# Graph attention by neighbour lists: a two-column copy ordered behind the norm factors' operation, and the first sort's triangle matmuls in the attention's PSUM tiles

## The chip, the cores and the metric

The kernel runs on one core of one Trainium2 chip. The metric is the device time of one execution in microseconds (us); smaller is better. Before the change three runs gave a median of 1821.51 us (1818.98 to 1823.71).

## What is computed

One layer of graph attention over 4096 nodes with 512 features, 8 heads of 64, and a dense 4096 x 4096 adjacency matrix of int32 in which a row holds some 9 ones on average. Cut to what matters:

```python
hs, ht = layer_norm(x), layer_norm(h_target)          # both [4096, 512]
q, k, v = ht @ Wq + bq, hs @ Wk + bk, hs @ Wv + bv    # 8 heads of 64
logits = where(adj != 0, q . k / 8, -1e30)            # per head
attn = softmax(logits) . v @ Wo + bo
ht = layer_norm(ht + attn)
ht = ht + gelu(ht @ W1) @ W2                          # 512 -> 2048 -> 512
out = layernorm(x + ht)
```

## The kernel before

The kernel does not form 4096 x 4096 logits. It turns each adjacency row into a short list of neighbours, sorts the rows by their number of neighbours, and for each tile of 128 rows gathers the keys and values of neighbour 0, 1, 2, ... from DRAM. A dense fallback (`general_path`) stands behind a flag at the end.

**The first stage** runs to about 300 us of the profile. Two kinds of work are interleaved in it.

- *Projections* (`project`, lines 864 to 960). For 16 groups of 256 rows of `x`: normalise (ScalarE, line 890), transpose on TensorE (line 904), scale into `hT` (ScalarE, line 914), multiply by Wk and Wv (TensorE, line 929), copy out of PSUM (ScalarE, line 931) and write 128 rows of keys and values to the DRAM table `kvd` (line 935, issued by ScalarE). An fp32 matmul appears in the profile as two passes.
- *Lists* (`edges`, lines 716 to 761). A row tile's adjacency comes in four quarters of 512 KB (line 713, issued by SyncE). ScalarE takes the sign of each entry (line 728), VectorE multiplies by an index and picks the largest by MAX8 (lines 733 and 735), then merges the candidates (lines 742 to 759) and SyncE writes the rest of them to DRAM (line 766). Each row tile has a record row with the degree, the row number, two norm factors and up to 24 neighbours (columns `DEG, TGT, ROW, RST, RST+1, E0...`).

After the first 16 row tiles (half "A") have lists, `prepare` calls `sort(0)` (lines 807 to 861): a counting sort by degree. A one-hot matrix `oh` of 48 bins is multiplied by a matrix of ones (line 838) for the running sums, which VectorE scans out of PSUM (line 839), and by a triangle `lower` (line 846) for the position inside a bin, which VectorE adds (line 847). The ranks come out of line 850, and GpSimd scatters the 16 record tiles by rank to DRAM (line 853). The second half of the rows, "B", is sorted during the attention by `sort(1)`, through the same lines.

**The attention stage** goes over 32 tiles of sorted rows. `prefetch` (line 979, on GpSimd) loads the sorted records of a tile into one of six `rec` buffers. `front` (lines 982 to 1016) gathers the target rows (line 966, GpSimd), copies degree and target row from the record to `tags` (line 993, VectorE, 128 x 2), applies a MAX with bypass to the two norm factors in the record (line 995, VectorE, in place), normalises with them (line 996, ScalarE), transposes (line 1000, TensorE), scales (line 1003, ScalarE), multiplies by Wq (line 1009, TensorE) and adds the bias (line 1014, VectorE). The operand `latest[-1]` on line 995 is not used in the value: it is there so that the operation comes after the tile it names, which is a `kvr` of the last two projection groups for the first two fronts and the logits `lg` of an attention step for the others. The attention itself gathers keys and values (line 966, 512 KB each), and multiplies by the query, reduces, exponentiates, weights and sums by TensorE transposes into the PSUM tile `cps` (lines 1218, 1223, 1227, 1182, 1190). `finish` divides and applies Wo (line 1113); `feed` is the feed-forward (lines 1323 and 1332); `end` normalises and scatters the output rows. `tags` is read by the gathers of `x` for the residual, by the output scatters (line 1300) and by `verdict` at the end of the attention.

**What sets the order.** `_weave` merges generators by the costs that they yield; that gives the order in which the program is written down. The build's scheduler then orders each engine's queue by its own model of times, moving instructions ahead where it takes their inputs to be there, unless an order is demanded. So a queue can hold an instruction long before its place in the text: the six copies of line 993 between 267 and 278 us belong to tiles 0 to 5, the operations of line 995 for tiles 2 to 5 come from 345 us on. An engine takes its queue in order.

**PSUM.** The pool `ps` has two tiles named `t` and two named `cps`[...]. In the first stage `t` is shared by the projections' transposes (line 899, every other pair of chunks) and the sort's matmuls; `cps` is used by the attention only.

Of the kernel before, what the change touches and what calls it, by code (L numbers as in the profile page):

```python
# [8 lines left out]
F32 = mybir.dt.float32  # L9
# [3 lines left out]
ALU = mybir.AluOpType  # L13
# [4 lines left out]
P = 128  # L18
# [359 lines left out]
DEG, TGT, ROW, RST, E0 = 0, 1, 2, 3, 5  # L378
# [65 lines left out]
def adj_resnorm_kernel(  # L444
# [33 lines left out]
    nc = tc.nc  # L478
# [54 lines left out]
    with tc.tile_pool(name="keep", bufs=1) as keep:  # L533
# [13 lines left out]
        tags = keep.tile([P, NT, 2], I32, name="tags")  # L547
# [3 lines left out]
        with ExitStack() as late:  # L551
# [3 lines left out]
            ps = late.enter_context(tc.tile_pool(name="ps", bufs=1, space=PSUM))  # L555
# [18 lines left out]
            def turn_of(name, places):  # L574
                turns[name] += 1
                return places[turns[name] % len(places)]
# [230 lines left out]
            def sort(part):  # L807

                i0, n = PARTS[part]
                me = slice(i0, i0 + n)  # L810
                pool, R = lp, Rs[part]
                nc.vector.tensor_reduce(deg[:, me], dpart[:, me, :], AX.X, ALU.add)
                nc.vector.tensor_copy(R[:, :, DEG], deg[:, me])
                dif, rank = tools[:, 928:928 + n], tools[:, 944:944 + n]
                ranki, b16 = tools[:, 960:960 + n].bitcast(I32), tools[:, 976:984].bitcast(BF16)
                nc.vector.scalar_tensor_tensor(dif, deg[:, me], float(RE), cnt[:, me], op0=ALU.min,
                                               op1=ALU.not_equal)
                nc.vector.tensor_reduce(bad[:, 1 + part:2 + part], dif, AX.X, ALU.max)
                nc.vector.tensor_scalar(dif, deg[:, me], 0.0, float(NB - 1), op0=ALU.max,
                                        op1=ALU.min)  # L820
                nc.vector.tensor_scalar(b16, dif, -1.0, float(NB - 1), op0=ALU.mult, op1=ALU.add)
                if part:
                    oh = turn_of("wide", wide).bitcast(BF16)
                else:
                    oh = wp.tile([P, NB * n], BF16, name="oh")
                oh = oh[:, :NB * n].rearrange("p (b i) -> p b i", b=NB)
                nc.vector.tensor_tensor(oh, b16.unsqueeze(1).to_broadcast([P, NB, n]),
                                        bins.unsqueeze(2).to_broadcast([P, NB, n]), ALU.is_equal)
                ohf = oh.rearrange("p b i -> p (b i)")
                pos = turn_of("wide", wide).bitcast(F32)  # L830
                pos = pos[:, :NB * n].rearrange("p (b i) -> p b i", b=NB)
                posf = pos.rearrange("p b i -> p (b i)")
                w = NB * n // 2
                yield 6.0
                for c in range(2):
                    sl = slice(c * w, (c + 1) * w)
                    pt = ps.tile([P, w], F32, name="t", bufs=2)
                    nc.tensor.matmul(pt, ones_bf, ohf[:, sl], start=True, stop=True)
                    nc.vector.tensor_tensor_scan(posf[:, sl], one_c.to_broadcast([P, w]), pt,
                                                 0.0 if c == 0 else posf[:, c * w - 1:c * w],  # L840
                                                 op0=ALU.mult, op1=ALU.add)
                yield 4.0
                for c in range(2):
                    sl = slice(c * w, (c + 1) * w)
                    pa = ps.tile([P, w], F32, name="t", bufs=2)
                    nc.tensor.matmul(pa, lower, ohf[:, sl], start=True, stop=True)
                    nc.vector.tensor_add(posf[:, sl], pa, posf[:, sl])
                nc.vector.tensor_mul(pos, pos, oh)
                nc.vector.tensor_reduce(rank, pos.rearrange("p b i -> p i b"), AX.X, ALU.add)
                nc.vector.tensor_copy(ranki, rank)  # L850
                yield 10.0
                for i in range(n):
                    ins = nc.gpsimd.indirect_dma_start(
                        out=recs_d[part][:, :],
                        out_offset=bass.IndirectOffsetOnAxis(ap=ranki[:, i:i + 1], axis=0),
                        in_=R[:, i, :], in_offset=None)

                    tc.declare_no_dep(ins.ins, group=f"scatter{part}", reason="other rows")
                    tc.add_to_no_dep_group(f"scatter{part}", ins.ins)
                    yield 3.0 if part else 1.3  # L860
                done.add(part)
# [101 lines left out]
            recs, tqs, h2Ts, done, ready, latest, newest = {}, {}, {}, set(), [], [], []  # L963

            def gather(dst, table, idx):
                nc.gpsimd.indirect_dma_start(  # L966
                    out=dst, out_offset=None, in_=table[:, :],
                    in_offset=bass.IndirectOffsetOnAxis(ap=idx, axis=0))
# [13 lines left out]
            def front(i, idle=0):  # L982


                rec = recs[i]
                tq = sp.tile([P, 2 * D], F32, name="tq", bufs=3)
                t = tq[:, :D]
                gather(t, h_target, rec[:, TGT:TGT + 1])
                for _ in range(1 + idle):
                    yield  # L990


                nc.vector.tensor_copy(tags[:, i, :], rec[:, DEG:TGT + 1])
                m = rec[:, RST:RST + 2].bitcast(F32)
                nc.vector.scalar_tensor_tensor(m, m, latest[-1], m, op0=ALU.bypass, op1=ALU.max)
                nc.scalar.activation(t, t, AF.Identity, bias=m[:, 1:2], scale=m[:, 0:1])
                yield
                pt = ps.tile([P, KC, P], F32, name="t", bufs=2)
                for kc in range(KC):
                    nc.tensor.transpose(pt[:, kc, :], t[:, kc * P:(kc + 1) * P], ident)  # L1000
                hT = tq[:, D:].rearrange("p (c t) -> p c t", c=KC)
                for kc in range(KC):
                    nc.scalar.activation(hT[:, kc, :], pt[:, kc, :], AF.Identity,  # L1003
                                         bias=b1r[:, kc:kc + 1], scale=s1c[:, kc:kc + 1])
                yield
                yield
                pq = ps.tile([P, D], F32, name="t", bufs=2)
                for kc in range(KC):
                    nc.tensor.matmul(pq, hT[:, kc, :], wq[:, kc, :], start=kc == 0,  # L1009
                                     stop=kc == KC - 1)  # L1010
                yield
                yield
                yield
                nc.vector.scalar_tensor_tensor(tq[:, :D], pq, HD ** -0.5, bqr,
                                               op0=ALU.mult, op1=ALU.add)
                tqs[i] = tq
# [32 lines left out]
            def begin(i, lead):  # L1049

                if i not in begun_fronts:
                    begun_fronts.add(i)
                    fronts[i] = front(i, 2 * lead + (2 if i > NA else 0))
                    step(fronts, i)
# [97 lines left out]
            def first_fronts():  # L1152

                for i in range(EARLY):
                    prefetch(i)
                for i in range(EARLY):
                    fronts[i] = front(i)
                    step(fronts, i)
                while not latest:
                    yield None  # L1160
                while fronts:
                    go_on()
                    yield 4.0
# [278 lines left out]
            def other_lists():  # L1442
                for cost in ed:
                    yield 1.5 * cost
                keep_rest()
                yield from sort(1)
# [38 lines left out]
```

## Time and profile before

| | |
|---|---|
| median of three runs | 1821.51 us (1818.98 to 1823.71) |
| the profiled execution's own time | 1820.38 us |
| its span, first to last instruction | 1818.6 us |
| TensorE (PE) busy | 1686.6 us, 93% of the span |
| VectorE (DVE) busy | 1435.0 us, 79% |
| ScalarE (ACT) busy | 1221.5 us, 67% |
| GpSimd (POOL) busy | 976.5 us, 54% |
| DMA | 463.26 MB, mean 255 GB/s |
| copy of line 993 | 32 times, median 168 ns |
| operation of line 995 | 32 times, median 212 to 218 ns |
| triangle matmul, line 846, first sort | 2 passes, 477 and 524 ns, at 235.8 and 237.8 us |

How to read it: "busy" adds up the instructions of an engine. In the lists of waits, "A <- B" means that engine A sat idle until B was done, and the number is that idle time. In the timeline a row has its start, its length, the engine, the line, the operation, tile written <- tiles read, a count, and in brackets the idle time just before it with what ended it. POOLq, SPq and ACTq are instructions that issue transfers, PEld is the loading of weights. In a table of stretches there are the busy time of each engine with its number of instructions, the clock that TensorE was granted (1.00 is full), the share of time in which the DMA engines were busy, and what they moved in GB/s.

### The profile page before, as it was taken

The page shows a single profiled execution, that of the slowest core. Times are in us where ns is not written, and L with a number is a line of the kernel's source. Part 1 is how long each engine was busy: PE and PEld are TensorE (multiplying, and loading weights), DVE is VectorE, ACT ScalarE, POOL GpSimd, SP SyncE. Part 2 cuts the span into 40 slices and gives each one's busy share as a digit, 9 for nine tenths or more (in the row PEclk, how much of TensorE's full clock was granted, in tenths as well). Part 3 has the DMA queues.
Part 4 walks back from the last instruction along what each step waited for, and adds up shares of the span by engine and source line. Part 5 has one row for each costly group of instructions (what it writes and reads, how often), then busy time and mean ns, then how long its engine had stood idle before and what let it go on. Part 6 is the DMA issues. An engine that isn't in the chain of part 4 may idle for free. (4 is left out here: it accounts for less than half of the span.)

```text
span 1818.6 us, 22965 instructions
## 1 busy us (share of the span) xinstructions
PE 1686.6 (93%) x7030; PEld 1100.9 (61%) x7030; DVE 1435.0 (79%) x2660; ACT 1221.5 (67%) x3119; POOL 976.5 (54%) x834
## 2 busy tenths in 40 slices
PE   7999975588999999999999989999999999999997
PEld 3444432466766666676776657666666666666664
DVE  6989866899999837787978989979879697988200
ACT  5867644486998645767878878877877576787311
POOL 1000143666465576676668788877575655764101
PEclk9999987598999999999999999999999999999999
DMA  9999958989887747677879878887786767774000
GB/s 345 366 389 370 346 171 304 405 284 324 292 303 234 238 141 269 227 267 263 289 259 316 296 258 277 261 291 266 241 268 206 262 222 242 247 248 152 18 6 26
DMA packets 140268, 463.26 MB, mean 255 GB/s; under 512 B 16500, under 2 KB 21672, under 8 KB 140136
## 3 DMA queue, kind: packets, MB, share of 16 engines
q0 software_dynamic: 96656, 342.64, 55.7%
q1 hardware_dynamic: 35664, 95.98, 15.0%
q10 hardware_dynamic: 7816, 23.08, 3.3%
q8 instruction: 58, 0.95, 0.2%
q14 instruction: 74, 0.61, 0.1%
HBM read 430.75 MB, written 30.89 MB: 254 GB/s over the span
## 5 line engine op out<-in xcount | busy, mean ns | idle before, releaser
L966 POOL DMA_INDIRECT kv<-kvd,rec x603 | 757.4, 1256 | 370.7 <-PE cps L1190 134.1
L1332 PE MATMUL po<-w,gt 128*128 128x512 f32 x1024 | 466.3, 598 | 6.6 <-ACT gt L1326 6.3
L1323 PE MATMUL pf<-h2T,w 128*128 128x256 f32 (+1 forms) x2176 | 466.5, 368 | 2.0 <-issue 1.7
L1323 PEld LDWEIGHTS pf<-h2T,w 128*128 128x128 f32 x2176 | 389.5, 191 | 66.9 <-issue 22.1
L1202 ACT ACTIVATE kv<-kv,pa 128x64 f32<-128x64 f32 x1520 | 391.0, 336 | 4.4
L1218 DVE TENSOR_TENSOR kv<-kv,tq 128x1536 f32<-128x1536 f32 (+2 forms) x211 | 352.0, 1678 | 51.0 <-DMA kv<-kvd,rec 48.4
L1223 DVE TENSOR_REDUCE lg<-kv 128x24 f32<-128x1536 f32 (+2 forms) x211 | 350.6, 1669 | 1.0
L1332 PEld LDWEIGHTS po<-w,gt 128*128 128x128 f32 x1024 | 188.9, 192 | 203.2 <-issue 195.2
L1190 PE MATMUL cps<-ident,kv 128*128 128x128 f32 x2008 | 267.5, 281 | 45.3 <-issue 22.7
L1190 PEld LDWEIGHTS cps<-ident,kv 128*128 128x128 f32 x2008 | 240.9, 146 | 112.7 <-issue 69.8
L1182 DVE TENSOR_TENSOR kv<-kv,p 128x1024 f32<-128x1024 f32 (+1 forms) x211 | 251.4, 1196 | 26.3 <-ACT p L1227 21.1
L687 POOL TENSOR_TENSOR n_rs<-n_ve,mhalf 128x2 f32<-128x2 f32 (+2 forms) x51 | 50.1, 983 | 329.8 <-DVE n_ve L680 154.5
L728 ACT ACTIVATE kv<-kv 128x1024 uint8<-128x1024 int32 x128 | 134.9, 1055 | 97.4 <-DMA kv<-in_adj_dram 49.3
L1326 ACT ACTIVATE gt<-pf 128x512 f32<-128x512 f32 x128 | 76.4, 597 | 97.1 <-PE pf L1323 74.9
L929 PE MATMUL pq<-wk,h2T 128*128 128x512 f32 x256 | 125.3, 634 | 12.3 <-ACT h2T L914 5.5
L735 DVE MAX8 cand<-kv 128x8 uint16<-128x103 uint16 (+1 forms) x640 | 133.6, 259 | 0.5
L1326 ACT ACT_TABLE_LOAD x103 | 132.1, 1283 | 1.7
L1009 PE MATMUL t<-wq,tq 128*128 128x512 f32 x256 | 117.4, 602 | 5.0 <-ACT tq L1003 4.3
L929 PE MATMUL pq<-wv,h2T 128*128 128x512 f32 x256 | 115.3, 593 | 0.6 <-ACT tq L931 0.6
L1113 PE MATMUL t<-wo,rb 128*128 128x512 f32 x256 | 115.2, 592 | 0.0
L1227 ACT ACTIVATE p<-lg 128x24 f32<-128x24 f32 (+2 forms) x179 | 39.1, 219 | 105.7 <-DVE lg L1223 83.3
L929 PEld LDWEIGHTS pq<-wk,h2T 128*128 128x128 f32 x256 | 50.4, 204 | 78.1 <-issue 59.0
(159 smaller groups left out, 1582.2 us busy)
## 6 DMA issues: line engine op xcount, KB each, us to landing
kv<-in_adj_dram SPq DMA_DIRECT2D x128, 512.0 KB
kvd<-tq ACTq DMA_DIRECT2D x24, 512.0 KB
kv<-kvd,rec POOLq DMA_INDIRECT x603
kv<-in_L_gnn_h_target_dram SPq DMA_DIRECT2D x32, 256.0 KB
kv<-in_x_dram SPq DMA_DIRECT2D x15, 512.0 KB
rest_d<-gid SPq DMA_DIRECT2D x32, 160.0 KB
w<-in_L_gnn_W_dram SPq DMA_DIRECT2D x4, 1024.0 KB
kvd<-kv ACTq DMA_DIRECT2D x8, 512.0 KB
```

What stands on the lines that cost most here:

```text
L728: nc.scalar.activation(sg, a, AF.Sign, accum_out=dpart[:, i, h:h + 1])
L735: nc.vector.max(cand[:, h * SQ + s, :], wd[:, w0:w1])
L929: nc.tensor.matmul(pkv, hT[:, kc, j * P:(j + 1) * P], w[:, kc, :], start=kc == 0, stop=kc == KC - 1)
L966: nc.gpsimd.indirect_dma_start(out=dst, out_offset=None, in_=table[:, :], in_offset=bass.IndirectOffsetOnAxis(ap=idx, axis=0))
L1182: nc.vector.tensor_tensor(v4, v4, p[:, j0:j0 + m, :].unsqueeze(3) .to_broadcast([P, m, H, HD]), ALU.mult)
L1190: nc.tensor.matmul(cps[:, c, :], kv[:, j, D + c * P:D + (c + 1) * P], ident, is_transpose=True, start=j0 + j == 0 and c == 0, stop=j0 + n ...
L1202: newest[:] = [nc.scalar.mul(v, v, pa[:, hd:hd + 1]).ins]
L1218: nc.vector.tensor_tensor(kv[:, :n, :D], kv[:, :n, :D], tq[:, :D].unsqueeze(1).to_broadcast([P, n, D]), ALU.mult)
L1223: nc.vector.tensor_reduce(lg[:, :n, :], kv[:, :n, :D].rearrange("p j (h d) -> p j h d", h=H), AX.X, ALU.add)
L1323: nc.tensor.matmul(pf[:, k, :], w1[(f0 + k) // KC][:, kc, (f0 + k) % KC * P:((f0 + k) % KC + 1) * P], h2T[:, kc, :w], start=kc == 0, stop= ...
L1326: nc.scalar.activation(gt, pf, AF.Gelu_apprx_tanh)
L1332: nc.tensor.matmul(po[j], gt[:, k, j * P:(j + 1) * P], w2[(f0 + k) // KC][:, (f0 + k) % KC, :], start=False, stop=f0 + k == FC - 1, skip_g ...
```

## The change

Two edits. In `front`, the copy of degree and target row (before: line 993, ahead of the operation on the norm factors) is written behind that operation and tied to it: `issue_after` adds an edge of order, on VectorE alone, from the operation to the copy. In `sort`, the PSUM tile of the triangle matmul takes the name `cps` in the first sort and keeps `t` in the second.

```diff
@@ sort
                     sl = slice(c * w, (c + 1) * w)
-                    pa = ps.tile([P, w], F32, name="t", bufs=2)
+                    pa = ps.tile([P, w], F32, name="t" if part else "cps", bufs=2)
                     nc.tensor.matmul(pa, lower, ohf[:, sl], start=True, stop=True)
                     nc.vector.tensor_add(posf[:, sl], pa, posf[:, sl])
@@ front
-                nc.vector.tensor_copy(tags[:, i, :], rec[:, DEG:TGT + 1])
                 m = rec[:, RST:RST + 2].bitcast(F32)
-                nc.vector.scalar_tensor_tensor(m, m, latest[-1], m, op0=ALU.bypass, op1=ALU.max)
+                tie = nc.vector.scalar_tensor_tensor(m, m, latest[-1], m, op0=ALU.bypass,
+                                                     op1=ALU.max)
+                with tc.issue_after(tie.ins):
+                    nc.vector.tensor_copy(tags[:, i, :], rec[:, DEG:TGT + 1])
                 nc.scalar.activation(t, t, AF.Identity, bias=m[:, 1:2], scale=m[:, 0:1])
```

## The prediction, written before the result

> **What bounds the kernel now.** I read the busy time by stretches first, because the shares of the whole span mix stages.
>
> ```profile
> 240.00:255.00 15.00, 15.00 (x42) 7.10 (x41) 12.66 (x55) 9.51 (x19) 9.49 (x10) 1.00 0.42 141
> 255.00:270.00 15.00, 10.72 (x31) 4.82 (x30) 3.05 (x18) 2.78 (x6) 10.80 (x14) 1.00 0.24 52
> 270.00:300.00 30.00, 25.68 (x56) 10.91 (x56) 22.40 (x99) 18.26 (x37) 3.73 (x5) 0.89 0.80 262
> 300.00:370.00 70.00, 28.42 (x124) 21.21 (x124) 55.70 (x84) 29.80 (x102) 48.44 (x39) 0.61 1.01 389
> 360.00:1740.00 1380.00, 1333.20 (x5970) 917.82 (x5969) 1139.65 (x1509) 992.42 (x2655) 886.03 (x734) 0.98 0.74 247
> 1740.00:1810.00 70.00, 65.49 (x290) 43.80 (x288) 3.41 (x14) 11.43 (x22) 4.67 (x6) 1.00 0.04 12
> ```
>
> Columns: stretch, length, PE, PEld, DVE, ACT, POOL, granted clock, DMA share, GB/s. From 360 us to the end PE is busy for 1333 of 1380 us, and in the last 70 us it works alone through the feed-forward that has queued up. So from 360 us on the end is set by PE's amount of work, and what an edit is worth is how much earlier PE gets that work going, plus what it takes from the 47 us that PE is idle there. In 300 to 370 us the limit is DMA (share 1.01): the first gathers run beside the last adjacency loads. In 255 to 270 us nothing looks full: DVE works 3 of 15 us, DMA a quarter. That hole is what I looked into next, by the waits at line 993 and the timeline.
>
> ```profile
> L993 DVE COPY tags<-rec x32: 151/168/428, 267.0 to 1449.2; 128x2 int32<-128x2 int32 x32
> its engine sat idle before it (us, times) until:
>   DMA rec<-rec: 48.1, 13
> ```
>
> ```profile
> 235.81 0.48 PE L846 MATMUL t<-oh,lower 128*128 128x384 bf16 x1 [6.05 <-DVE kv L839]
> ...
> 264.91 2.73 POOL L979 DMA_DIRECT2D rec<-rec  x5 [1.76 <-DMA rec<-R,kv]
> 266.95 0.17 DVE L993 COPY tags<-rec 128x2 int32<-128x2 int32 x1 [12.14 <-DMA rec<-rec]
> ...
> 268.73 1.06 ACT L728 ACTIVATE kv<-kv 128x1024 uint8<-128x1024 int32 x1 [12.22 <-DVE cand L735]
> ...
> 270.87 5.16 PE L929 MATMUL pq<-wk,h2T 128*128 128x512 f32 x8 [5.15 <-ACT h2T L914]
> ...
> 278.06 0.17 DVE L993 COPY tags<-rec 128x2 int32<-128x2 int32 x1 [2.77 <-DMA rec<-rec]
> ...
> 278.78 0.34 DVE L995 SCALAR_TENSOR_TENSOR rec<-rec,kv 128x2 f32<-128x2 f32 x2
> ...
> 279.88 1.36 PE L1000 MATMUL t<-ident,tq 128*128 128x128 f32 x8 [0.42 <-ACT tq L996]
> ...
> 294.62 0.33 ACTq L935 DMA_DIRECT2D kvd<-kv  x1
> ...
> 301.63 0.94 POOL L966 DMA_INDIRECT kv<-kvd,rec  x1 [26.97 <-DMA kvd<-kv]
> ```
>
> The reader is to see a chain. The copy stands in DVE's queue from 254.8 us and waits 12.14 us for a record whose load POOL issues at 264.91. Behind it stands the list work (line 735), so ACT's next sign (line 728) waits 12.22 us; behind that in ACT's queue stand the copies and scalings of the projections, so PE waits 5.15 us for `hT`. The last key-value write (294.62) is late, and the first gather (301.63) waits for it. By the list of waits DVE loses 14.9 us of the 48.1 before 302 us, and 33.2 us in 11 waits between 540 and 1450 us. Apart from this, PE stands 6.05 us before the first triangle matmul, until the scan of line 839 frees the tile `t`.
>
> **What the Trainium skill says.** "PSUM — Partial Sum Buffer", section "Engine vs sequencer instructions": the queues of ScalarE, VectorE and GpSimd are strict FIFO, and matmuls start in program order. The trace agrees: three queues stand still behind one copy of 168 ns. "DMA: Bandwidth & Descriptors", "Anatomy of one DMA — SWDGE (gpsimd) path": a transfer issued by GpSimd takes about 2.0 us and its bytes at 436 GB/s. Here the first 14.5 KB record took at most 2.0 us (264.91 to 266.95), but the one issued at 271.53 was there only at 278.06, 6.5 us, with the DMA engines at 0.8 to 1.0: load decides. "TensorE: Matmul & The Clock Gate", "What's actually happening": after an idle window of some 3.4 us the clock halves until PE has been busy as long. Agrees: after the 5.15 us the clock was 0.66 in 270 to 275 us, and eight passes took 5.16 us where they take 3.60 elsewhere.
>
> **The change, part by part**, against the profiled execution's 1820.38 us (span 1818.6 and 1.8 around it; the median of the runs is 1.1 higher).
>
> *1. Copies of the first stage behind the tie.* Six copies leave the stretch 254 to 279 us, and with them 14.9 us of DVE waits. The operation of line 995 needs the same record, so part of the wait stays. Between the first copy and that operation DVE did 278.78 - 266.95 - 2.77 = 9.1 us of work. Starting at 254.8 it is there at 263.9 at the earliest, and the record lands at 266.95: 3 us of waiting in place of 14.9. Of the gain PE had hidden the larger part, as it held matmuls until 265.7. It gets back 5.15 us of waiting and 5.16 - 3.60 = 1.56 us of slow clock, so it reaches the fronts' transposes (line 1000) at 279.88 - 6.7 = 273.2. Their data: the target rows are requested at 267.94 and 269.26; 256 KB by the DMA page's price take 2.6 us (an estimate), so 271.9 for the second, 0.8 us of line 996, 272.7. The two nearly meet; with some DMA load I take 274, a gain of 5.9. From line 1000 to the last write it is 14.7 us, with a wait of ACT of 2.61 us for an adjacency quarter (at 286.98) of which PE's own matmuls (done by about 286.4) would leave 1.6 us to gain at the copy of 288.04; the loads run ahead once DVE and ACT don't stand still, and I take 1.1. Sum **-7.0** at the last write and at the first gather, 7.0 us behind it. Ends: 3 (the record and the target rows come later under the load that now fills the hole) to 9.5 (6.7 + 1.6 and a shorter write).
>
> *2. Adjacency loads out of the gathers' way.* In 255 to 270 us DMA moved 52 GB/s, in the 15 us before 141: 1.3 MB of loads go back into the hole. They lie in the stretch at 389 GB/s now, 3.4 us of it. Value **-2**, ends 0 to -3.4.
>
> *3. Triangle matmuls in `cps`.* The wait of 6.05 us for the scan falls; `cps` is free, as its first use is at 319.85. What is late next: the same line 847 needs the scan's result, so the ranks come no sooner (DVE has no idle time there but 0.5 us), and the record stays at 267. PE gets up to 6 us ahead in the projections, but then meets the fronts at line 1000, which I put at 274 by their data. What is left is ACT's idle 5.42 us for `pq` and some 3 us of DVE waiting for ACT at 246 to 253. Value **-1.5**, ends 0 to -6. Its matmuls and adds are the same in number; moved past them in PE's queue are only projection matmuls.
>
> *4. Copies of the attention.* 33.2 us of DVE waits, all after 540 us, where PE has feed-forward queued: after the wait of 5.39 us at 758.61 and that of 5.68 at 676.74 PE shows none. The cover is the PE queue; gone, these would cost their whole length. PE's one wait for DVE in the stretch of the longest ones is 3.53 us at 723.39. Value **-1**, ends 0 to -4.
>
> *5. What is added.* The edge has no semaphore: tie and copy are on one engine. Behind the tie a copy of 0.17 us delays ACT's line 996 by nothing, as it stands after the tie. The tie now is the first reader of the record, but it was placed up to 170 us behind the copy (last starts 1623.4 and 1449.2), so in the attention the record has long landed. Readers of `tags`: residual gathers and scatters of a tile come after its front, and the two at 272.42 and 273.71 may move some us on a POOL that is idle until 301.63. Cost **0**, ends 0 to +1; no reason excludes a small loss.
>
> Sum: -7 - 2 - 1.5 - 1 = -11.5, so 1808.9 for the profiled execution and **1810** for the median. All ends together: -22.9 (1799) and about -2 to -3 (1819).
>
> **Rivals.**
>
> *The wait moves to the tie.* If the scheduler puts the tie where the copy was, DVE still stands until 267 for the record. For it: the same input, the same model that takes it to be early. Against it: the tie also needs a `kvr` of a late projection, and stood 9.1 us of work behind. Then steps 1 and 2 shrink to what the later copies cost (2.77 us) and step 3: about -3, 1818.5.
>
> *More comes back.* DVE is busy 98% from 350 to 540 us and PE idles 14 us in 360 to 480. If the lists' lead and the PSUM edit both count in full: all upper ends, 1799.
>
> *Slower: the fronts hold the projections.* PE is in order, and line 1000 stands before the last wk and wv matmuls. In the hole the scatters, records and target rows had the DMA engines nearly to themselves. If the adjacency loads that return make each of these three steps as long as the record issued at 271.53 (6.5 us), the record is issued at 264.91 + 4.7 = 269.6 and lands at 276.1, target rows land by 277 + 1.3 + 6.5 = 284.9, line 1000 starts at 285.7: 5.8 us later than now, and DVE stands at the tie besides. Time 1827.5. It decides from three steps of some 15 us in sum, where now records and rows need about 7.
>
> **How the numbers follow.** Forecast 0.63; wait moves 0.17; more comes back 0.12; slower 0.08. This kernel's measurement tells 0.3% (5.5 us) from no change. The forecast's own cases run from 1802 to 1817 and lie past that bound but for 0.04; the first rival is within it but for 0.03: faster 0.59 + 0.03 + 0.12 = 0.74, same 0.19, slower 0.07. The range 1799 to 1820 leaves out the slower case, half of "more comes back" and a little of the first rival, some 0.17.
>
> **What would show it.** Right: no wait over some 4 us on DVE between 254 and 270; DMA share in 255 to 270 near 0.7; line 1000 at about 274; last key-value write at about 287.6, first gather near 294.6; no wait before line 846; waits for `rec` at the copy gone everywhere. Wrong: a wait for `rec` of 8 us or more at line 995's place, line 1000 at or after 280, or a first gather that comes 7 us sooner with an end that doesn't, in which case PE's idle time after 360 us has grown.

## The result, and the profile after

The changed kernel takes 1814.79 us (median of six runs, 1811.19 to 1818.93), the kernel before beside it 1822.36 us (1818.98 to 1830.21). The ratio is 0.9952 with a 95% interval of 0.9933 to 0.9972: faster by about half a per cent. A second measurement of the same kernel gave 0.9945 (0.9925 to 0.9965). The profiled execution took 1811.19 us, its span is 1809.4 us, 9.2 us shorter than before. From line 993 on, lines stand two further down: the operation on the factors is 994, the tied copy 997, its ScalarE step 998, the fronts' transposes 1002.

The stretches of the changed kernel, columns as before:

```profile
240.00:255.00 15.00, 15.00 (x42) 7.10 (x41) 14.93 (x64) 8.08 (x15) 9.21 (x10) 1.00 0.44 145
255.00:270.00 15.00, 11.02 (x26) 4.56 (x24) 8.18 (x40) 6.27 (x12) 9.86 (x13) 0.99 0.67 197
270.00:300.00 30.00, 18.01 (x40) 8.15 (x40) 18.49 (x79) 15.68 (x31) 7.76 (x9) 0.78 0.72 230
300.00:370.00 70.00, 31.49 (x137) 24.03 (x138) 57.84 (x81) 31.00 (x110) 49.06 (x39) 0.60 1.00 389
360.00:1740.00 1380.00, 1336.51 (x5973) 921.73 (x5972) 1134.38 (x1507) 993.12 (x2656) 886.28 (x731) 0.98 0.73 246
```

The hole at 255 to 270 us is filled: VectorE works 8.2 us where it worked 3.1, and DMA moves 197 GB/s where it moved 52. But in the next 30 us PE works only 18.0 us, against 25.7 before. The timeline of the changed kernel shows why:

```profile
228.83 0.49 PE L846 MATMUL cps<-oh,lower 128*128 128x384 bf16 x2
...
266.53 2.73 POOL L979 DMA_DIRECT2D rec<-rec  x5 [3.01 <-DMA rec<-R,kv]
...
268.84 0.22 DVE L994 SCALAR_TENSOR_TENSOR rec<-rec,kv 128x2 f32<-128x2 f32 x1 [6.78 <-DMA rec<-rec]
268.98 0.28 DVE L997 COPY tags<-rec 128x2 int32<-128x2 int32 x1
...
273.93 1.11 PE L1002 MATMUL t<-ident,tq 128*128 128x128 f32 x4 [7.91 <-ACT tq L998]
...
282.38 1.06 ACT L728 ACTIVATE kv<-kv 128x1024 uint8<-128x1024 int32 x1 [4.05 <-DMA kv<-in_adj_dram]
...
290.03 0.33 ACTq L935 DMA_DIRECT2D kvd<-kv  x1
...
296.81 0.96 POOL L966 DMA_INDIRECT kv<-kvd,rec  x1 [20.42 <-ACT kv L728]
```

The wait before the triangle matmul is gone. The record's load is issued 1.6 us later than before, as the scatters ahead of it take longer; the tie now waits 6.78 us for it. PE comes to the fronts' transposes early and stands there 7.91 us (0.42 us before) until ScalarE has normalised the first target rows, which POOL requests at 269.56. The transposes start at 273.93, 5.95 us sooner than before. The last key-value write is sooner by 4.6 us only, since ScalarE waits for an adjacency quarter on the way, and the first gather by 4.8 us. No copy waits for a record any more; the answer on line 997 has no row under the idle time:

```profile
L997 DVE COPY tags<-rec x32: 156/165/354, 269.0 to 1615.4; 128x2 int32<-128x2 int32 x32
its engine sat idle before it (us, times) until:
who waited for it (us, times):
```

Where the 9.2 us of the span come from can be split by PE, whose 7030 passes are the same in both kernels:

```profile
PE 1681.5 (93%) x7030; PEld 1101.4 (61%) x7030; DVE 1435.1 (79%) x2660; ACT 1221.1 (67%) x3119; POOL 979.8 (54%) x834
```

PE is busy 5.1 us less (1686.6 before) and outside its busy time 4.1 us less (132.0 to 127.9). The same passes in less busy time fit less time at a slow clock, so that a wait of PE costs more than its length; an experiment below shows one such place. The second trace of the change splits alike (1680.3 busy, 127.7 outside). That of the fastest kernel below does not (1685.6 and 121.1), so the split holds for these traces and is no rule.

### The profile page after: what moved, and what is told of

It is laid out like the page before. It is cut to its first block, busy times and chain, and to the rows that moved or that the text cites. A ratio compares the mean times of both kernels' runs of the same rounds, so it can differ in the third digit from the quotient of the medians.

```text
span 1809.4 us, 22969 instructions
## 1 busy us (share of the span) xinstructions
PE 1681.5 (93%) x7030; PEld 1101.4 (61%) x7030; DVE 1435.1 (79%) x2660; ACT 1221.1 (67%) x3119; POOL 979.8 (54%) x834
## 5 line engine op out<-in xcount | busy, mean ns | idle before, releaser
L929 PE MATMUL pq<-wk,h2T 128*128 128x512 f32 x256 | 121.3, 619 | 8.3 <-ACT tq L931 5.7
```

The costliest lines, as they stand in the source:

```text
L929: nc.tensor.matmul(pkv, hT[:, kc, j * P:(j + 1) * P], w[:, kc, :], start=kc == 0, stop=kc == KC - 1)
```

## The experiments

**Theory.** After the result I held that the ties give nearly the whole gain and the PSUM edit little; that the waits in the attention are worth 1 to 3 us; and that PE's wait at the fronts' transposes holds the first stage back. **Rivals:** the PSUM edit carries a third or more; the attention gives half of the gain; ScalarE's waits for adjacency quarters hold the first stage. The runs bear out the first part of the theory and, for the attention, the rival.

Each ratio is to the kernel before, run beside it (medians 1826.41, 1824.52 and 1824.35 us in the three sets of runs). Single executions of one kernel differ by up to 14 us (before: 1819.13 to 1833.41), so ratios count, and a trace is used for where a wait stands.

| kernel | ratio, 95% interval |
|---|---|
| ties, no PSUM edit | 0.9942 (0.9921 to 0.9962) |
| PSUM edit only | 1.0003 (0.9989 to 1.0017) |
| ties of tiles 6 to 31 only | 0.9975 (0.9964 to 0.9986) |
| ties of tiles 0 to 5 only | 0.9999 (0.9989 to 1.0009) |
| the change again | 0.9945 (0.9925 to 0.9965) |
| change, waits back from tile 6 on | 0.9988 (0.9978 to 0.9998) |
| change, wait back at tile 13 | 0.9973 (0.9962 to 0.9984) |
| change, waits back at tiles 14 to 21 | 0.9942 (0.9922 to 0.9962) |
| change, waits back from tile 26 on | 0.9962 (0.9950 to 0.9975) |
| change, fronts tied to group 15 | 0.9946 (0.9928 to 0.9964) |
| change, fronts tied to the last projection | 0.9934 (0.9921 to 0.9947) |
| the same, list rests written later | 0.9947 (0.9933 to 0.9962) |

### Which of the two edits

Ties without the PSUM edit:

```diff
-                    pa = ps.tile([P, w], F32, name="t" if part else "cps", bufs=2)
+                    pa = ps.tile([P, w], F32, name="t", bufs=2)
```

> The copies behind the tie as in the change, but the first sort's triangle matmuls in the tile t as before. Theory: the tie is nearly all of the gain. TensorE's wait of 6 us before line 846 comes back, but the records of the first tiles (requested at 266.5 us in the changed kernel) hold the fronts anyway, so the first gather stays within 1.5 us of the changed kernel's 296.8 us; time 5 to 8 us below before. Rival: the PSUM edit carries a third or more: first gather at 299 us or later, time 2 to 4 us below before.

And the kernel before with the PSUM edit alone:

```diff
-                    pa = ps.tile([P, w], F32, name="t", bufs=2)
+                    pa = ps.tile([P, w], F32, name="t" if part else "cps", bufs=2)
```

> The triangle matmuls of the first sort in cps, the copies as before. Theory: no wait before line 846, but the copy still stands in VectorE's queue until the record is there (over 12 us of waiting), TensorE waits for hT as long as it has got ahead (10 us or more at about 266 us), and the first gather comes at 300 to 302 us; time 0 to 2 us below before. Rival (PSUM edit worth a third or more): first gather at 299 us or sooner, time 3 to 5 us below before.

Measured: 0.9942 and 1.0003. The ties give it all, and the PSUM edit by itself nothing. Neither expectation for the ties held whole: the time fell by more than the 5 to 8 us of the theory (0.9942 is 10.6 us), while the first gather came at 300.63, as late as the rival said. The list of waits of the kernel with the PSUM edit only, from 215 to 302 us, tells where PE's lead went:

```profile
DVE tags L993 <- DMA rec<-rec: 16.9, 2, 14.3
...
PE pq L929 <- ACT h2T L914: 12.5, 1, 12.5
```

PE reaches the copy's stall sooner and waits 12.5 us there, where it waited 5.15. In the trace with ties only, the record is late and PE meets the fronts at 278.84, almost as late as before (279.88):

```profile
267.44 2.73 POOL L979 DMA_DIRECT2D rec<-rec  x5 [3.96 <-DMA rec<-R,kv]
...
278.84 1.97 PE L1002 MATMUL t<-ident,tq 128*128 128x128 f32 x8 [4.61 <-ACT tq L998]
...
300.63 0.94 POOL L966 DMA_INDIRECT kv<-kvd,rec  x1 [23.23 <-ACT kv L728]
```

Over the traces taken, the first gather is at 294.8 to 299.4 us (mean 297.7) in the six of the kernels with both edits in the first stage and the fronts tied as in the change, at 300.6 and 300.0 with the early ties and no PSUM edit, 301.6 and 302.1 with neither, 303.9 with the PSUM edit alone. So both edits bring this moment 4.2 us forward against neither, the ties alone about 1.6; the times of the whole, 0.9942 and 0.9945, do not show the difference.

### Early or late ties

The change without its PSUM edit, with only the tiles from 6 on tied, whose copies stand in the attention, and the copies of the others ahead of the operation as before:

```diff
+                if not i >= 6:
+                    nc.vector.tensor_copy(tags[:, i, :], rec[:, DEG:TGT + 1])
                 m = rec[:, RST:RST + 2].bitcast(F32)
...
-                with tc.issue_after(tie.ins):
-                    nc.vector.tensor_copy(tags[:, i, :], rec[:, DEG:TGT + 1])
+                if i >= 6:
+                    with tc.issue_after(tie.ins):
+                        nc.vector.tensor_copy(tags[:, i, :], rec[:, DEG:TGT + 1])
```

> PSUM tile as before; the copies of tiles 0 to 5 stay ahead of the operation on the factors, those of tiles 6 to 31 are tied. Theory: the first stage is that of before (a wait of about 12 us at the copy, first gather at about 301.6 us); the 33 us of waits in the attention are gone and are worth little, since TensorE has feed-forward queued: 1 to 3 us below before. Rival: the attention part is half of the gain, 4 us or more below before.

The other half, with `i < 6` in both places:

> The counterpart of the run with late ties: only the copies of tiles 0 to 5 are tied, those of tiles 6 to 31 stay ahead of the operation on the factors; PSUM tile as before. Theory: the two parts add up. All ties gave -0.58%, the late ones -0.25%, so the early ones give about -0.33%: 4 to 8 us below before, with a wait of 0 to 7 us at the first tie in place of 14.9 at the copies. Rival: the first stage gives little (the first gather was only 1 us sooner in the trace with all ties and the old PSUM tile): 0 to 2 us below before, and the two parts do not add up.

The late ties give 0.9975, some 4.6 us, which is the rival's figure and not the theory's 1 to 3 us. The early ones give 0.9999: the six copies on which the prediction rests its largest term are worth nothing measurable alone. The two do not add up to the 0.9942 of both. On top of the late ties the early ones are worth some 6 us (0.9975 to 0.9942), on top of the early ones the late ones some 10 (0.9999 to 0.9942). The end of the next section shows where the early gain goes when it stands alone.

The change run again, and the change with the waits put back: a further copy of the same two columns, which nothing reads, free to go ahead as before:

> The changed kernel itself once more, beside the others on one chip. Theory: -0.5 to -0.6% against before, within 1.5 us of the run with all ties and the old PSUM tile (the PSUM edit is worth nothing). Rival: the PSUM edit adds to the ties though it gave nothing alone: 3 us or more below that run.

```diff
+                if i >= 6:
+                    nc.vector.tensor_copy(sp.tile([P, 2], I32, name="idle"), rec[:, DEG:TGT + 1])
                 m = rec[:, RST:RST + 2].bitcast(F32)
```

> The changed kernel with an extra copy of the same two columns to an unused tile, untied, for tiles 6 to 31: it stands where the copies stood before, and waits for the record. Theory: the waits themselves cost time in the attention: 25 to 40 us of VectorE waits for rec come back, and the time rises by 3 to 6 us over the changed kernel (26 copies of 0.17 us by themselves are 4 us of VectorE, which is not the bound there). Rival: what helped in the attention is only that the scheduler ordered the queues in another way: the waits come back and the time stays within 1.5 us.

0.9945 and 0.9988. With the first stage as the change has it, the waits alone take back 0.0043, some 7.8 us, more than the 3 to 6 us expected. The copies that were added last 0.17 us each; eight of them cost nothing in a run below. From its list of waits:

```profile
DVE idle L992 <- DMA rec<-rec: 34.6, 11, 9.4
```

### Which of the waits

Three kernels put back part of them. The edit is the one just shown, with `i == 13`, with `14 <= i < 22` and with `i >= 26`.

> The changed kernel with one untied copy more, of two columns, for tile 13 only: it stands in VectorE's queue ahead of the second sort's scans of line 839. The run with such copies for all tiles from 6 on gave 0.9988 of the time before, the changed kernel 0.9945. Theory 'two places': this one copy waits 8 to 10 us for its record, TensorE waits 4 to 6 us for the tile t behind the scans, the stretch from the second to the third group's first scatter is 93 us or more instead of 88.4, and the ratio is about 0.9970. Rival 'it adds up over all the waits': one wait of 9 of the 34.6 us gives a quarter of the 0.0043, so about 0.9956. Rival 'covered': TensorE's queue takes it up later, ratio 0.9945.

> The changed kernel with untied copies more for tiles 14 to 21 only, between about 680 and 1025 us, where the waits for a record were 15.3 us in 8 waits with all of them back. Theory 'two places': TensorE has work queued there, the stretches of the groups in 660 to 1050 us stay within 1.5 us in sum of those of the changed kernel, ratio about 0.9948. Rival 'it adds up over all the waits': 15.3 of 34.6 us of waits give 0.44 of the loss of 0.0043, ratio about 0.9964.

> The changed kernel with untied copies more for tiles 26 to 31 only, between about 1270 and 1460 us, where three of them waited 9.9 us with all of them back. Theory 'two places': the stretch from 1401 to 1484 us of the kernel before is 82 to 83 us again instead of 79 to 80, the one from 1228 to 1315 up to 5 us longer, and the ratio is about 0.9967 to 0.9985. Rival 'it adds up over all the waits': 9.9 of 34.6 us, ratio about 0.9957. Rival 'covered': 0.9945.

One wait of 9.3 us at tile 13 costs 0.0028 (0.9973 against 0.9945, some 5 us), seven of 15.5 us in the middle nothing (0.9942), three of 9.8 us near the end 0.0017 (0.9962, some 3 us). The sum, 0.0042, is near that of all together (0.0043). The intervals of single pairs still touch (tile 13 and the change at 0.9962 to 0.9965), the last pair overlaps widely. "It adds up over all the waits" fails at the middle and at tile 13, where it said 0.9964 and 0.9956. "Two places" holds for these two; near the end the measured 0.9962 lies below its 0.9967 to 0.9985 and nearer to the 0.9957 of its rival, so the time alone does not show the second place, and the traces below have to. One expectation was too narrow: the middle, between two groups' first output scatters at 654.4 and 1044.5 us, took 390.1 us, 3.2 more than in the change's two traces (386.9 each), where 1.5 was expected; kernels without such copies there lie between 384.9 and 390.8, so this tells nothing.

How one wait comes to cost 5 us is in the timeline of the kernel with the wait at tile 13:

```profile
595.20 0.60 POOL L979 DMA_DIRECT2D rec<-rec  x1
...
600.65 0.17 DVE L992 COPY idle<-rec 128x2 int32<-128x2 int32 x1 [9.31 <-DMA rec<-rec]
...
619.88 0.95 DVE L839 TENSOR_TENSOR_SCAN kv<-one_c,t 128x384 f32<-128x384 f32 x1
...
620.97 1.09 PE L1142 MATMUL t<-ident,h 128*128 128x128 f32 x4 [3.83 <-DVE kv L839]
```

The copy stands in VectorE's queue ahead of the second sort's scans (line 839). The first scan starts 8.0 us after its matmul of line 838 (611.89), where it takes 1.7 us in the change (609.16 to 610.83). Until the scans have read the tile `t`, PE's transposes of line 1142 can't have it: they wait 3.83 us, **twenty microseconds after the copy**. Then the clock falls. The stretches of this kernel, and of the changed one at the same work:

```profile
615.00:620.00 5.00, 2.15 (x16) 1.75 (x15) 5.00 (x7) 4.96 (x11) 4.09 (x4) 1.00 0.87 270
620.00:625.00 5.00, 3.16 (x10) 1.96 (x10) 4.96 (x5) 4.95 (x18) 4.39 (x3) 0.52 0.92 327
625.00:630.00 5.00, 4.24 (x9) 2.06 (x9) 3.38 (x3) 4.94 (x11) 1.27 (x2) 0.50 0.71 237
```

```profile
606.00:611.00 5.00, 5.00 (x24) 3.35 (x23) 5.00 (x7) 4.96 (x11) 3.96 (x4) 1.00 0.88 278
611.00:616.00 5.00, 5.00 (x32) 4.04 (x30) 4.97 (x5) 4.95 (x18) 2.91 (x2) 1.00 0.69 248
616.00:621.00 5.00, 3.69 (x15) 1.91 (x15) 1.65 (x2) 4.94 (x12) 2.16 (x3) 1.00 0.66 197
```

The first column after the length is PE's busy time: 2.15 and 3.16 of 5 us with the wait, 5.00 without, and for ten microseconds the granted clock is 0.50 to 0.52 in place of 1.00. This is what the Trainium skill says in "TensorE: Matmul & The Clock Gate", section "What's actually happening": the clock is halved after an idle window of about 3.4 us and given back after as long a busy one. The trace agrees on the half (0.50); the slow spell here lasted about 10 us, with PE busy 3.2 to 4.2 of each 5 us. From the second group's first output scatter to the third's it takes 94.4 us, where the change takes 88.5. In that stretch PE stands 5.45 us against 1.31, 4.1 more; and its 393 passes take 0.2263 us each, the change's 402 take 0.2169, which makes 3.7 us more (roughly, as the mix differs).

**Why early and late ties do not add up.** The same place shows it. In the kernel before, the wait at tile 13 is shorter, and PE waits for the scans twice, each time for less than 2 us:

```profile
593.42 0.61 POOL L979 DMA_DIRECT2D rec<-rec  x1
...
598.53 0.17 DVE L993 COPY tags<-rec 128x2 int32<-128x2 int32 x1 [5.91 <-DMA rec<-rec]
...
620.02 0.63 PE L1140 MATMUL t<-ident,h 128*128 128x128 f32 x4 [1.77 <-DVE kv L839]
...
622.50 1.12 PE L1140 MATMUL t<-ident,h 128*128 128x128 f32 x4 [1.85 <-DVE kv L839]
```

With the early ties alone, whose lines stand one to five further down, it looks like this:

```profile
596.46 0.61 POOL L979 DMA_DIRECT2D rec<-rec  x1
...
601.85 0.24 DVE L994 COPY tags<-rec 128x2 int32<-128x2 int32 x1 [9.22 <-DMA rec<-rec]
...
623.30 1.01 PE L1145 MATMUL t<-ident,h 128*128 128x128 f32 x4 [4.86 <-DVE kv L839]
...
626.28 1.12 PE L1145 MATMUL t<-ident,h 128*128 128x128 f32 x4 [1.97 <-DVE kv L839]
```

VectorE comes to the copy at 592.6 us in both, but with the early ties the record's load is issued 3.0 us later. The stretch between the second and the third group's first scatter takes 94.2 us in place of 87.6. It takes 94.2 to 95.4 us in the three traces with early ties and this wait, 87.6 and 87.9 in the two with the wait and without early ties, and 85.8 to 88.8 in the nine without the wait. For about the same number of passes, the late ties save 1.8 us here without the early ones (87.6 to 85.8) and 7.1 us with them (94.2 to 87.1). So alone, the early ties lose here what they gain before. Why the load comes later is not shown.

Near the end, the stretch between two such scatters that ends at 1476 us in the change takes 78.7 to 80.3 us in the nine traces without copies that wait there, and 82.0 to 83.1 us in the five with such copies (82.6 in the run with the last waits only, 83.1 in the kernel before), with 343 to 345 passes of PE in every one. So the second place is there, worth some 3 us. In the timeline of the kernel before, the place looks like this:

```profile
1449.18 0.33 DVE L993 COPY tags<-rec 128x2 int32<-128x2 int32 x1 [3.04 <-DMA rec<-rec]
...
1455.10 0.22 ACT L1236 ACTIVATE p<-lg 128x24 f32<-128x24 f32 x1 [5.37 <-DVE lg L1223]
...
1461.84 1.09 PE L1190 MATMUL cps<-ident,kv 128*128 128x128 f32 x8 [0.67 <-DVE kv L1186]
...
1464.78 0.86 PE L1096 MATMUL t<-ident,rb 128*128 128x128 f32 x4 [1.85 <-ACT h2T L1144]
```

The products and sums of lines 1218 and 1223 come late, ScalarE's exponentials wait, and PE stands 12 to 16 us after the copy. That these waits follow from the copy is read from their order in the timeline.

### What holds the first stage

PE's wait at the fronts stands ahead of the last projections. Two kernels tie the fronts to a later projection: to group 15 in place of 14 and 15, and to its second half only.

```diff
-                    if n >= 14:
+                    if n >= 15:
```

> The changed kernel, with the first two fronts' operation on the factors waiting for a key-value tile of the last projection group (n >= 15) in place of the last two (n >= 14). Theory: what is left of the hole is the fronts: TensorE stands 7.9 us at line 1002 in front of the last projections, VectorE 6.8 us at the tie. One step later in the order both shrink to 3 us or less, the last key-value write comes 3 to 6 us sooner than 290.0 us and so does the first gather (291 to 294 us); time 3 to 6 us below the changed kernel, 10 to 13 below before. Rival: ScalarE's waits for adjacency quarters (12 us in four waits between 215 and 302 us) are what holds the last writes: first gather no sooner than 295.5 us, time within 2 us of the changed kernel.

```diff
-                    if n >= 14:
+                    if n == 15 and j == 1:
```

> The changed kernel, with the first two fronts' operation waiting for the very last key-value tile (n == 15 and j == 1), which puts line 1002 behind the last projections in TensorE's queue and leaves the rest of that queue as it is. Theory: the fronts' data held the last projections; TensorE goes through them at once, the last key-value write comes at 280 to 286 us (290.0 in the changed kernel), the first gather at 287 to 293, the queries still in time, and the whole is 3 to 8 us below the changed kernel. Rival: ScalarE's waits for adjacency quarters and its own queue hold the last copies, or the queries are late: first gather no sooner than 295 or first product of line 1220 no sooner than 307; within 2 us of the changed kernel.

With the first edit the transposes still stand ahead of the last projections, and everything comes later than in the change:

```profile
283.76 1.11 PE L1002 MATMUL t<-ident,tq 128*128 128x128 f32 x4 [10.07 <-ACT tq L998]
...
295.29 0.33 ACTq L935 DMA_DIRECT2D kvd<-kv  x1
...
302.06 0.95 POOL L966 DMA_INDIRECT kv<-kvd,rec  x1 [19.74 <-DMA kvd<-kv]
```

The first gather is some 5 us later than in the change and as late as in the kernel before (301.63), and still the ratio is 0.9946, as the rival had it. In this trace the lag is gone by the output scatter at 837.20 us (837.39 in the change). With the ties alone it is much the same: 300.63 and 0.9942. **By these two runs the gain does not rest on an earlier first gather.** The second edit moved the transposes behind the last projections, where they start at 286.62. The last write still came at 288.82 (290.03 in the change), the first gather at 296.9 (296.81): the fronts were not what held this stage. Its list of waits in 250 to 300 us:

```profile
ACT kv L728 <- DMA kv<-in_adj_dram: 18.1, 7, 5.1
DVE kv L733 <- ACT kv L728: 9.5, 6, 3.7
```

ScalarE takes over: 18.1 us in seven waits for adjacency quarters. At 0.9934 it is the fastest kernel measured, but the change's interval covers it, so it isn't shown to be better. Between 240 and 300 us SyncE waits 21.4 us for VectorE before its writes of the list rests, with adjacency loads behind them. So, on top of this kernel:

```diff
-                    if h == 1:
+                    if h == 3:
                         keep_rest()
```

> The run in which only the very last projection names the tile for the fronts (0.9934 of the time before, last key-value write at 288.8, first gather at 296.9), with one edit more: the write of a row tile's list rests is put on SyncE's queue two quarters later, so that fewer adjacency loads stand behind a write that waits for VectorE. Theory 'SyncE's order holds the first stage': the write's waits of 12.9 us in 240 to 300 us fall below 5, ScalarE's waits for adjacency in 250 to 300 us fall from 18.1 to under 8, the last key-value write comes by 285, the first gather by 293, ratio about 0.991 to 0.992. Rival 'the adjacency's transfers themselves hold it': ScalarE's waits stay at 12 us or more and the gather at 296 to 298, ratio 0.9934. A loss is possible where the next row tile's lists wait for the buffer that the write still reads: then VectorE has new waits for a DMA in the list lines 742 to 759 and the ratio is above 0.995.

0.9947, the first gather at 297.0. The edit did little of what it should: SyncE still waits 17.6 us for VectorE before these writes, and ScalarE still 17.8 us for quarters:

```profile
ACT kv L728 <- DMA kv<-in_adj_dram: 17.8, 6, 5.5
```

Whether the order of SyncE's queue or the transfers themselves make the quarters late **stays open**.

## Why the prediction was right, and where it was not

The time (1814.79) lies in the range and on the side that was forecast. The gain is some 8 to 10 us by the two ratios, where the sum said 11.5. That it came near is luck: two errors offset each other. Steps 1 to 3, put at -10.5, are worth 0 to 6 us, by whether the late ties are there; step 4, put at -1, is worth 5 to 10.

**Step 1, copies of the first stage, -7.0 at the first gather.** The mechanism is there: the hole fills, and line 1000 (now 1002) starts at 273.93 where the prediction said 274. That needs both edits: with ties alone it is 278.84. "A gain of 5.9" was 5.95. The term that failed is the next one, "the loads run ahead once DVE and ACT don't stand still, and I take 1.1": from there to the last write it took 16.1 us, not 13.6, with ScalarE waiting 4.05 us for a quarter at 282.38 and 12.2 us in all before the first gather, where it waited 8.2 before. "3 us of waiting" at the tie was 6.78: the record came 1.9 us later under the load, and VectorE was at the tie 1.8 us sooner (262.06, not 263.9). The target rows, which the prediction estimated at 2.6 us, took up to 3.5 (269.56 to the start of line 998 at 273.06). The gather's gain was 4.8 us in this trace, some 4 us in the mean of six. The premise behind the whole term fails too, that the end moves by as much as the first gather: the early ties alone give 0.9999, the first stage of the change with the later waits put back 0.9988, 0.4 to 4 us; on top of the late ties the early ones give some 6 us; and with the first gather as late as before (302.06) the ratio is still 0.9946.

**Step 2, adjacency out of the gathers' way, -2.** Not seen where it was put. 300 to 370 us is as full as before (share 1.00, 389 GB/s), and from the first gather to the first output scatter it takes 187.9 us (187.2 before; 186.6 to 188.4 over all traces). A shortening of 2.2 us stands later, between the first two scatters (80.5 us in place of 82.7, VectorE busy 79.9 in place of 81.8). It is there (80.4 to 80.6) in eight traces with all tiles tied, not with only early or only late ties (82.7 each), nor with all waits put back (82.0), nor in the last experiment (82.2). PE has 350 passes in it in the change and 367 before, and 402 against 377 in the stretch behind it, so a part of the shortening is work that moved on. Why it takes both is open.

**Step 3, triangle matmuls, -1.5.** The reasoning that the ranks come no sooner was right, and so was "meets the fronts". Alone the edit gives 1.0003; its part shows only together with the ties, in the first gather.

**Step 4, copies of the attention, -1.** This is the term that was mis-sized. Late ties alone give 0.9975, 4.6 us; putting the waits back costs 7.8 us, where the wait at tile 13 is longer (9.3 us) than it was before (5.91). On top of the early ties the late ones give some 10. So the step is worth about 5 to 10 us, more than its upper end of 4. "The cover is the PE queue" holds for the middle, 15.5 us of waits that cost nothing. It fails at two places. The prediction looked for a PE wait beside each copy's wait and took 3.53 us at 723.39 for the only one; the waits that matter stand 12 to 24 us behind the copies, under the name of another line (line 839's scans; lines 1096 and 1190), and it counted their length without the slow clock that follows. The list of waits of the kernel before did have the row, `PE t L1140 <- DVE kv L839: 3.6` (the 1.77 and 1.85 us shown above, behind the longest of these waits); it was not followed back to the copy. The Trainium skill, "Perfetto Trace Analysis", section "Identifying Performance Opportunities", says to take the gaps of the engine that should be full and ask what each one waits for; from PE's 3.6 us that way leads through the scans to the copy, while the prediction started at the copies. By the traces this place cost the kernel before only some 2 us (87.6 against 85.8); it would have cost 7 once the early copies were tied, and the prediction priced its steps one by one.

**Step 5, nothing for what is added.** The ties of the attention have no wait for a record, as the prediction said. One thing is added that it left out: gathers of keys and values behind the tied copy, by the trace, 8.6 us in 9 waits on POOL, none before:

```profile
POOL kv L966 <- DVE tags L997: 8.6, 9, 4.1
```

Six of the nine are the 0.3 us that stand between most gathers anyway, the longest is 4.10 at 1286.27; no run takes them away alone, so their cost is not known.

**The rivals.** "The wait moves to the tie" was right in its mechanism for one tile, 6.78 of the 14.9 us, and wrong for the rest. "The fronts hold the projections" named what did happen: record and target rows late under the load, and PE standing 4.3 to 9.7 us at the fronts in six traces. It did not decide: with the fronts moved away the last write came 1.2 and 2.3 us sooner than in the change's two traces, and the gather at the same time.

**Open.** Early ties (0.9999) and late ties (0.9975) together give 0.9942, some 6 us more than their sum. The traces place some 5 us of it at tile 13 and 2.2 between the first two scatters. They are single executions: the one with the early ties took 1830.13 us, where that kernel's median is 1823.59. Why the load at tile 13 is issued later with the early ties, and by what path the early ties help once the late ones are there, is not shown.

## What to carry to other kernels

An instruction of 0.2 us that may be moved ahead in an in-order queue, and whose input comes by DMA, can cost what the work behind it costs: tie it behind the first instruction that needs the same data anyway. Price two such edits together as well as one by one; here each alone gave 0 and 5 us, and both gave 10. To judge the cover, don't look for idle time of the bounding engine beside the stall; follow the queue behind the stalled instruction to whatever holds a shared buffer, and look there, in this kernel 12 to 24 us later. A hole filled early in a kernel fills with other transfers too, so price the next wait before counting the gain.

## What was not expected of the hardware

- A gap of PE of 3.83 us and a shorter one behind it brought 10 us at a clock of 0.50 to 0.52, and the slow spell cost about as much as the gaps (3.7 and 4.1 us, worked out above). In the kernel before, two gaps of 1.77 and 1.85 us at the same work brought 0.70 in 620 to 625 us and 0.96 in the next five.
- The blocking copy lasts 0.17 us in the trace while it holds its engine for 9.31. The Trainium skill, "Perfetto Trace Analysis", section "Per-instruction lifecycle: what the profiler-reported window actually captures", says that waits for semaphores lie outside the recorded window; the trace agrees, and a list by busy time does not bring such an instruction to the top.
- One record's load, of 14.5 KB, took at most 2.0 us in the hole of the kernel before and about 5.4 us in the kernel with the wait at tile 13 (issue at 595.20, copy at 600.65), where the DMA share was 1.00 from 595 to 600 us.
